# A graph-attention kernel: 18 targets instead of 20 summed early, and eight projection steps for each instead of seven

## The chip, the cores and the metric

The kernel runs on one core of a Trainium2 chip. The metric is the device time of one execution in microseconds (us); the time before is the median of six executions. The engines are TensorE (PE: matmuls, and PEld: its weight loads), VectorE (DVE), ScalarE (ACT), GpSimd (POOL) and SyncE (SP). Each engine works through its own queue of instructions in order, and waits for others by semaphores. Transfers (DMA) are issued from the queues of SP, ACT and POOL and share 16 DMA engines. The schedule in this kernel is written by hand: the order in which the Python code emits instructions is the order in each queue.

## What is computed

Two layers of graph attention over 3327 nodes with 1024 features, each followed by a residual and a normalisation. The adjacency matrix is sparse (about 16 neighbours for each node).

```python
def _L0_gnn_ref(x, adj, W, a_src, a_dst):          # 8 heads of 128
    h = (x @ W).reshape(C, H, D)
    e = alpha_src[:, :, None] + alpha_dst[:, None, :]
    e = where(e >= 0, e, 0.2 * e); e = where(adj[None] == 0, -inf, e)
    attn = softmax(e, axis=-1)
    return einsum('hij,hjd->hid', attn, h_heads)   # concatenated heads
def _L1_gnn_ref(input, adj, W, a1, a2):            # one head of 1024
    h = input @ W
    e = leaky_relu(h @ a1 + (h @ a2).T, 0.2); scores = where(adj > 0, e, neg)
    return relu(softmax(scores, axis=1) @ h)
x = _layernorm(x + _L0_gnn_ref(x, adj, ...))
x = _layernorm(x + _L1_gnn_ref(x, adj, ...))
```

## The kernel before

Nodes are cut into 26 tiles of 128 rows (`NT = 26`, `NTH = 13`). A tile of nodes that receives is called a target. The kernel makes, for each target, lists of its neighbours on DVE, and then gathers the neighbours' rows from a table in HBM with indirect transfers on POOL's queue. The neighbours of a target are put into blocks: blocks 0 and 1 hold neighbours out of tiles 0 to 12 (the near half), blocks 2 and 3 those out of tiles 13 to 25, and an end block holds what didn't fit. A block is four gathers of 128 rows, the end block one.

**Projection.** For every tile, PE makes h = x W in three pieces of columns, eight matmuls each (L578); ACT copies them out and SP stores the row of 1048 values (1024 features, a one for each head and two factors for each head) into the table `h0_d`. Tile t+1's third piece, with the scores, comes before its first two. Beside the matmuls run two generators, moved on by `pace()`, which is called after every second matmul of a piece, so 12 times for a tile: `listing()` makes the neighbour lists (seven steps a tile, paced by a line over the slots), and from tile 13 on `sums_so_far()`, one step at each pace.

**Early sums.** `sums_so_far()` computes the near half of layer 0's sums for the first `EARLY` = 20 targets, while the projection of tiles 13 to 25 goes on: the near half's rows are all in the table by then. There are 11 steps of preparation. Then, for each target and each of its two near blocks, three steps: `fetch(n + 2)` puts out the gathers of the block two ahead into one of three buffers (`near0`, `near1`, `far`; L696), `marks` (L704) and `weights` (L713, L714, L717) are DVE work, `sums` is PE work in two halves of 16 matmuls (L726; each appears as two instructions), and ACT scales the target's own row (L755), which an ACT-issued transfer brought. After the second block `settle` (L759) adds the three banks of sums to the own row on DVE, SP loads the lists of the target after the next, and a seventh step ends the target. SP stores the row into `half_d` in the next target. At target 12 `own_terms(NTH, EARLY)` makes the own factors of the rest. The loop also fetches the near blocks of target `EARLY` for the next stage. After the last tile, a loop runs out what is left of both generators.

**Rest of layer 0.** `sparse()` goes through all 26 targets. An early target needs its two far blocks and the end block (9 gathers) and loads its half sum from `half_d`; the 6 late targets need all five blocks (17 gathers) and load the own row from `h0_d`. The order is one late target, then five early ones, four times, then the last two late targets. Gathers (L1082) go out as the five block buffers come free. DVE makes weights (L1157 to L1160), PE sums (L1183, end block L1175, own rows L1172), then follow the division, the normalisation and the store of y.

**Layer 1** gathers rows of y the same way (17 gathers a target), sums on PE (L1283) and multiplies by the second weights (L1315).

`FIRST` names the targets whose lists hold a valid row in every place, as they fill buffers for the first time: 0, 1 and the first two late ones.

Of the kernel before, what the change touches and what calls it, by code (L numbers as in the profile page):

```python
# [26 lines left out]
def kernel(  # L27
# [35 lines left out]
    NTH = NT // 2  # L63
# [23 lines left out]
    HB = EB // 2  # L87
    HG2 = HB * P
    THR = NTH * P
    EARLY = NTH + 7  # L90
    FIRST = 0, 1, EARLY, EARLY + 1
    XN, XR, XL = 1, 2, 2 + H
    XB = XL + KMAX
# [41 lines left out]
    row_d = [scratch.tile([1, P], F32, name=f"row_d{t}") for t in range(NT)]  # L135
    half_d = [scratch.tile([P, DW], F32, name=f"half_d{t}") for t in range(EARLY)]
    io_t = const.tile([P, P], F32, name="io_t")
# [5 lines left out]

    own_e = const.tile([P, EARLY, H], F32, name="own_e")

# [396 lines left out]
    with ExitStack() as own, tc.manual_schedule():  # L542
# [140 lines left out]
        def sums_so_far():  # L683

            src = [near[0], near[1], far]
            k = EARLY * HB % 3
            src = src[-k:] + src[:-k] if k else src
            bound = nc.gpsimd.to_reg(THR - 1)

            def fetch(n):  # L690
                s, b = divmod(n, HB)
                if s > EARLY:
                    return
                for g in range(NG):
                    k = b * NG + g
                    nc.gpsimd.indirect_dma_start(  # L696
                        out=src[n % 3][:, g, :], out_offset=None, in_=h0_d[:THR, :],
                        in_offset=bass.IndirectOffsetOnAxis(ap=idx[:, s, k : k + 1], axis=0),
                        bounds_check=bound, oob_is_err=False,
                    )  # L700

            def marks(s):
                oh = part.sbuf("oh", [P, HB * NG, GT], 2)
                nc.vector.tensor_tensor(  # L704
                    oh, io_t[:, :GT].unsqueeze(1).to_broadcast([P, HB * NG, GT]),
                    tgt[:, s, : HB * NG].unsqueeze(2).to_broadcast([P, HB * NG, GT]), OP.is_equal,
                )
                return oh

            def weights(val, b, re, oh):  # L710
                blk = slice(b * NG, (b + 1) * NG)
                w = part.sbuf("w", [P, NG, H], 4)
                nc.vector.tensor_tensor(w, val[:, :, DW : DW + H], re[:, blk, :], OP.mult)  # L713
                nc.vector.tensor_tensor(w, w, val[:, :, DW + H :], OP.max)  # L714
                e = part.sbuf("e", [P, H * P], 2).rearrange("p (g h t) -> p g h t", g=NG, h=H)
                wide = [P, NG, H, GT]
                nc.vector.tensor_tensor(  # L717
                    e, oh[:, blk, :].unsqueeze(2).to_broadcast(wide), w.unsqueeze(3).to_broadcast(wide), OP.mult
                )
                return e  # L720

            def sums(acc, val, b, e, heads_):
                vals = val[:, :, :DW].rearrange("p g (h d) -> p g h d", h=H)
                for h in heads_:
                    for g in range(NG):
                        nc.tensor.matmul(  # L726
                            acc[h // 3][g * GT : (g + 1) * GT, h % 3, :], e[:, g, h, :], vals[:, g, h, :],
                            start=b == 0 and h in HEADS, stop=b == HB - 1 and h + 1 in HEADS,
                        )

            def listed(s):
                re = part.sbuf("re", [P, HB * NG, H], 3)
                nc.sync.dma_start(re, re_d[s][:, : HB * NG, :])
                return re

            def own_terms(lo, hi):

                mid = ph.sbuf("bits", [P, 8, KMAX], 1, dt=I32).rearrange("p a b -> p (a b)").bitcast(F32)
                m, e = (hi - lo) * H, own_e[:, lo:hi, :]
                mids = [mid[:, n * m : (n + 1) * m].rearrange("p (t h) -> p t h", h=H) for n in range(2)]  # L740
                for n, scale in enumerate((1.0, SLOPE)):
                    nc.scalar.activation(mids[n], sd0[:, lo:hi, 1, :], AF.Exp, scale=scale)
                nc.scalar.activation(e, sd0[:, lo:hi, 0, :], AF.Exp, scale=1 - SLOPE)
                nc.vector.tensor_tensor(e, e, mids[0], OP.mult)
                nc.vector.tensor_tensor(e, e, mids[1], OP.max)
                nc.vector.tensor_tensor(e, e, loop[:, lo:hi].unsqueeze(2).to_broadcast([P, hi - lo, H]), OP.mult)

            def own_row(s):
                if s < EARLY:
                    nc.scalar.dma_start(own_rows[s % 3], h0_d[s * P : (s + 1) * P, :DW])  # L750

            def scale(s, heads_):
                for h in heads_:
                    d = by_head(own_rows[s % 3])[:, h, :]
                    nc.scalar.activation(d, d, AF.Copy, scale=own_e[:, s, h : h + 1])  # L755

            def settle(s, acc, n):
                d = by_head(own_rows[s % 3])[:, HEADS[n] : HEADS[n + 1], :]
                nc.vector.tensor_tensor(d, acc[n], d, OP.add)  # L759

            def store(s):
                nc.sync.dma_start(half_d[s], own_rows[s % 3])
# [19 lines left out]
            for s in range(EARLY):  # L782
                acc = [part.bank("L", [P, HEADS[n + 1] - HEADS[n], DH1], "part") for n in range(3)]
                for b in range(HB):
                    n = s * HB + b
                    val, last = src[n % 3], b == HB - 1
                    if n:
                        fetch(n + 2)
                    yield
                    if last and s + 1 < EARLY:  # L790
                        oh = marks(s + 1)
                    yield
                    if s and b == 0:
                        store(s - 1)
                    sums(acc, val, b, e, range(H // 2))
                    scale(s, range(b * H // 2, b * H // 2 + 2))
                    yield
                    sums(acc, val, b, e, range(H // 2, H))
                    if last:
                        res.pop(0)  # L800
                    if n + 1 < EARLY * HB:
                        e = weights(src[(n + 1) % 3], (b + 1) % HB, res[0], oh)
                    scale(s, range(b * H // 2 + 2, (b + 1) * H // 2))
                    if last:
                        own_row(s + 2)
                if s == NTH - 1:
                    assert scored.issuperset(range(EARLY))
                    own_terms(NTH, EARLY)
                for n in range(3):
                    settle(s, acc, n)  # L810
                if s + 2 < EARLY:
                    res.append(listed(s + 2))
                yield
# [113 lines left out]
        for t in range(3, NT):  # L927
# [24 lines left out]
            if t == NTH:  # L952
                soon.append(sums_so_far())
# [641 lines left out]
```

## Time and profile before

| | |
|---|---|
| median of 6 executions | 1775.02 us (1770.69 to 1779.56) |
| profiled execution | 1768.09 us, span 1766.4 us, mean granted clock 0.945 |
| busy share of the span | PE 87%, PEld 49%, DVE 65%, POOL 59%, ACT 27% |
| transfers | 595.95 MB, mean 337 GB/s; 459.23 MB on POOL's queue |
| first early gather / first gather of the next stage | 233.1 us / 575.4 us |
| last matmul of the projection ends | 569.3 us |
| first gather of layer 1's rows | 1033.2 us |
| ends of the sums of the late targets | 621.6, 724.0, 829.5, 930.8, 1038.3, 1059.7 us |

The profile is one execution, and its times are counted from the start of the span. Busy shares are averages over stages that differ, so each stage has to be read by itself; a line such as L726 is a line of the kernel. A wait line reads "engine line <- who released it: us in total, times, longest". Idle time in front of an instruction is put down to the semaphore that came last.

### The profile page before, as it was taken

What the parts mean: (1) busy time and instruction counts of PE and PEld (TensorE: products, weight loads), DVE (VectorE), ACT (ScalarE), POOL (GpSimd) and SP (SyncE); (2) the same over time, 40 slices, a digit from 0 to 9 for tenths busy, and PEclk for the clock granted to TensorE, in tenths of its full rate; (3) what the DMA queues carried; (4) which work ended last, traced back from release to release, by engine and by line L of the source; (5) the groups of instructions that cost most, each with busy time, mean ns of one, the idle gap of its engine ahead of it and who ended that gap; (6) DMA issues with size and microseconds to landing.
All of it is one profiled execution on the core that took longest, in us unless ns stands there. A gap on an engine that the chain in (4) does not pass through costs nothing.

```text
span 1766.4 us, 33978 instructions
## 1 busy us (share of the span) xinstructions
PE 1543.8 (87%) x12635; PEld 859.8 (49%) x12635; DVE 1147.2 (65%) x3111; ACT 474.1 (27%) x1396; POOL 1045.1 (59%) x1311
## 2 busy tenths in 40 slices
PE   9799989999998478777767674999999999999998
PEld 5566656565565345454544441444444444444443
DVE  6699998898886778786877763343434444343443
ACT  5677753343333112222221221111101111110110
POOL 4433256676665666666666664666666666666650
PEclk9899999999899698898988997999999999999999
DMA  7699989999899999999999997999999999999980
GB/s 184 121 160 168 185 267 375 363 398 396 328 380 348 369 376 409 394 399 382 396 395 374 407 387 288 371 381 380 381 355 386 381 371 373 368 386 388 357 334 36
DMA packets 190320, 595.95 MB, mean 337 GB/s; under 512 B 37914, under 2 KB 47924, under 8 KB 190146
## 3 DMA queue, kind: packets, MB, share of 16 engines
q0 software_dynamic: 131056, 459.23, 73.2%
q1 hardware_dynamic: 56052, 123.63, 19.1%
q10 hardware_dynamic: 3038, 10.83, 1.6%
q8 instruction: 102, 1.67, 0.4%
q14 instruction: 72, 0.59, 0.1%
HBM read 593.53 MB, written 54.99 MB: 367 GB/s over the span
## 4 chain that ended last, share of the span: by engine, by line
PE 51%; DVE 11%; DMA 10%; issue 7%; ACT 1%; POOL 0%; DVEq 0%; SPq 0%; another core or an unknown queue 0%; POOLq 0%; ACTq 0%
PE mm L1315 21%; PE acc L1283 15%; PE acc L1183 7%; DMA src<-h_d,idx 3%; PE acc L1172 2%; PE acc L1175 2%; PE mm L578 1%; PE tr L206 1%; PE part L726 1%; DMA re_d<-re 1%; DMA near<-h_d,idx 1%; DMA own<-h_d 1%; DVE e L1160 1%; DVE top L322 1%; DVE pr L1048 1%
## 5 line engine op out<-in xcount | busy, mean ns | idle before, releaser
L578 PE MATMUL mm<-wt,xT 128*128 128x384 f32 (+1 forms) x1248 | 410.5, 473 | 0.6 <-issue 0.5
L1315 PE MATMUL mm<-wt,xT 128*128 128x512 f32 x832 | 388.8, 605 | 1.6 <-issue 1.4
L1082 POOL DMA_INDIRECT src<-y_d,idx x248 | 250.1, 1009 | 142.8 <-PE acc L1283 63.9
L578 PEld LDWEIGHTS mm<-wt,xT 128*128 128x128 f32 x1248 | 228.9, 193 | 125.8 <-issue 31.5
L1318 DVE SCALAR_TENSOR_TENSOR o<-mm,y 128x512 f32<-128x512 f32 x52 | 36.0, 692 | 336.3 <-PE acc L1283 131.4
L1315 PEld LDWEIGHTS mm<-wt,xT 128*128 128x128 f32 x832 | 149.4, 189 | 202.1 <-issue 197.2
L1082 POOL DMA_INDIRECT near<-y_d,idx x168 | 169.3, 1008 | 83.9 <-PE acc L1283 33.7
L1082 POOL DMA_INDIRECT src<-h_d,idx x152 | 159.5, 1049 | 89.2 <-PE acc L1183 42.6
L1183 PE MATMUL acc<-src,e 128*32 128x129 f32 x2432 | 135.2, 309 | 64.9 <-issue 43.8
L1283 PE MATMUL acc<-src,es 128*32 128x341 f32 x1488 | 138.2, 471 | 25.3 <-DVE es L1274 20.8
L696 POOL DMA_INDIRECT near<-h_d,idx x112 | 122.8, 1096 | 53.8 <-issue 24.0
L1082 POOL DMA_INDIRECT near<-h_d,idx x96 | 104.9, 1092 | 66.5 <-PE acc L1183 36.6
L1183 PEld LDWEIGHTS acc<-src,e 128*32 128x32 f32 x2432 | 87.4, 122 | 113.8 <-issue 84.3
L1183 PE MATMUL acc<-near,e 128*32 128x129 f32 x1664 | 86.4, 300 | 51.1 <-issue 31.7
L1160 DVE TENSOR_TENSOR e<-oh,way 128x1024 f32<-128x1024 f32 x90 | 109.9, 1221 | 26.6 <-PE acc L1183 14.7
L1297 ACT ACTIVATE z<-y,ri 128x342 f32<-128x342 f32 (+1 forms) x78 | 39.5, 570 | 318.0 <-issue 107.6
L209 ACT ACTIVATE xT<-tr 128x512 f32<-128x512 f32 x52 | 31.1, 597 | 268.6 <-PE tr L206 151.2
L1283 PEld LDWEIGHTS acc<-src,es 128*32 128x32 f32 x1488 | 51.0, 112 | 101.2 <-issue 61.5
L1183 PEld LDWEIGHTS acc<-near,e 128*32 128x32 f32 x1664 | 58.1, 119 | 81.6 <-issue 68.0
L1283 PE MATMUL acc<-near,es 128*32 128x342 f32 (+1 forms) x1008 | 88.7, 455 | 3.1 <-DVE es L1274 2.0
L696 POOL DMA_INDIRECT far<-h_d,idx x56 | 63.4, 1133 | 36.6 <-PE part L726 21.2
L415 ACT ACTIVATE junk<-ad 128x1664 uint8<-128x1664 uint8 x52 | 83.1, 1597 | 6.9 <-POOL ad L404 5.3
(236 smaller groups left out, 2336.3 us busy)
## 6 DMA issues: line engine op xcount, KB each, us to landing
y_d<-y SPq DMA_DIRECT2D x26, 514.0 KB
y<-y_d SPq DMA_DIRECT2D x26, 514.0 KB
xT<-in_x_t_dram SPq DMA_DIRECT2D x26, 512.0 KB
h_d<-ht SPq DMA_DIRECT2D x25, 524.0 KB
y<-in_x_dram SPq DMA_DIRECT2D x25, 512.0 KB
out_dram<-o SPq DMA_DIRECT2D x25, 512.0 KB
ad<-in_adj_dram POOLq DMA_DIRECT2D x25, 415.9 KB
own<-half_d SPq DMA_DIRECT2D x20, 516.0 KB
```

Source lines behind the costliest of these rows:

```text
L415: nc.scalar.activation(junk, ad[:, n * THR : (n + 1) * THR], AF.Copy, accum_out=self.d[:, n : n + 1])
L578: nc.tensor.matmul(accs[t, c], xT[t][:, k, :], wt[:, k, CUTS0[c] : CUTS0[c + 1]], start=k == 0, stop=k == KT - 1)
L696: nc.gpsimd.indirect_dma_start(out=src[n % 3][:, g, :], out_offset=None, in_=h0_d[:THR, :], in_offset=bass.IndirectOffsetOnAxis(ap=idx[:, ...
L1082: nc.gpsimd.indirect_dma_start(out=s[:, g, :w], out_offset=None, in_=table[:n, :], in_offset=bass.IndirectOffsetOnAxis(ap=idx[:, t, b * NG ...
L1160: nc.vector.tensor_tensor(e, oh.unsqueeze(2).to_broadcast([P, ng, H, wide]), wp.unsqueeze(3).to_broadcast([P, ng, H, wide]), OP.mult,)
L1172: nc.tensor.matmul(self.acc[n].rearrange("p h d -> p (h d)"), ident, part, start=False, stop=False)
L1175: nc.tensor.matmul(self.acc[h // 3][:, h % 3, :], e[:, 0, h, :], rowsof[:, 0, h, :], start=False, stop=h + 1 in HEADS,)
L1183: nc.tensor.matmul(self.acc[h // 3][g * GT : (g + 1) * GT, h % 3, :], e[:, g, h, :], rowsof[:, g, h, :], start=j == 0 and h in HEADS, stop ...
L1283: nc.tensor.matmul(self.acc[c][to, :m], es[:, g, :], s[:, g, CUTS[c] : CUTS[c + 1]], start=b == 0, stop=b == EB,)
L1297: nc.scalar.activation(z[:, cut], self.res[:, cut], AF.Copy, scale=ri[:, 1:2])
L1315: nc.tensor.matmul(acc, xT[:, k, :], wt1[:, k, half], start=k == 0, stop=k == KT - 1)
L1318: nc.vector.scalar_tensor_tensor(o[:, half], acc, 0.0, res[:, half], op0=OP.max, op1=OP.add)
```

## The change

The number of targets summed early goes from 20 to 18, and a further `yield` in `sums_so_far()` makes the adding up (`settle`) and the load of the next lists a step of their own, one pace after the second half of the second block's matmuls: eight steps for a target.

```diff
     THR = NTH * P
-    EARLY = NTH + 7
+    EARLY = NTH + 5
     FIRST = 0, 1, EARLY, EARLY + 1
...
                 if s == NTH - 1:
                     assert scored.issuperset(range(EARLY))
                     own_terms(NTH, EARLY)
+                yield
                 for n in range(3):
                     settle(s, acc, n)
                 if s + 2 < EARLY:
                     res.append(listed(s + 2))
                 yield
```

By `EARLY`, targets 18 and 19 become late ones. The rest of layer 0 then has eight late and 18 early targets, in the order of one late and three early ones, six times, then the last two late ones. The buffers of the early sums are rotated so that target 18's near blocks fall into `near0` and `near1` (the rotation is by 36 mod 3 = 0 in place of 40 mod 3 = 1).

## The prediction
> **What bounds the kernel now.** I read the stages first: busy time of each engine by stretch, with the stretches cut where the kernel changes its work. The span has four parts: projection alone (to about 246 us), projection with early sums beside it (to about 570), the rest of layer 0 (to about 1065), layer 1 (to the end). Columns: busy us of PE, weight load, DVE, ACT and POOL (each with its count), granted clock, DMA share, GB/s.
>
> ```profile
> core 0: us, PE busy (x) PEld busy (x) DVE busy (x) ACT busy (x) POOL busy (x), PEclk, DMA share, GB/s
> 170.00:246.00 76.00, 74.40 (x312) 48.62 (x312) 70.59 (x206) 57.32 (x157) 26.05 (x66) 1.00 1.00 189
> ...
> 276.50:415.25 138.75, 128.59 (x1486) 82.17 (x1490) 124.64 (x332) 52.37 (x218) 96.03 (x131) 0.99 1.01 385
> 415.25:551.80 136.55, 125.45 (x1406) 78.94 (x1402) 116.75 (x311) 48.35 (x195) 84.25 (x109) 0.96 0.96 365
> 276.50:551.80 275.30, 254.05 (x2884) 161.11 (x2888) 241.40 (x642) 100.72 (x411) 180.28 (x239) 0.98 0.98 375
> 551.80:575.00 23.20, 18.20 (x214) 11.13 (x214) 11.79 (x33) 8.78 (x40) 11.22 (x14) 0.94 0.91 326
> 575.00:1065.00 490.00, 350.89 (x4709) 236.32 (x4709) 369.99 (x920) 102.77 (x228) 313.45 (x296) 0.87 1.01 390
> ```
>
> With early sums PE is 92% busy, DVE 88% and DMA moves 375 GB/s: three resources are near full together. In the rest of layer 0 PE is 72% and DVE 76% busy while 390 GB/s flow. The DMA share of 1.00 says little: it is 1.00 at 189 GB/s too. GB/s decides.
>
> Next, who waits in the stage with early sums (us in total, times, longest).
>
> ```profile
> DVE w L713 <- DMA near<-h_d,idx: 5.9, 6, 3.0
> DVE kq L523 <- ACT xs L509: 3.7, 1, 3.7
> ...
> DVE w L713 <- DMA far<-h_d,idx: 2.4, 2, 1.3
> DVE ad L759 <- ACT ad L755: 1.8, 1, 1.8
> DVE ad L759 <- PE part L726: 1.7, 2, 1.5
> ```
>
> DVE waits for gathered rows in 8 of its about 34 blocks, 8.3 us out of 275. The chain of waits in this stretch runs mostly along DVE (listing steps and weights), in shorter pieces along PE, and three times over a transfer (7.6, 9.7 and 9.5 us). In the order of time, DVE instructions follow each other at 0.02 to 0.05 us; one tile of projection takes 27.5 us (ten copies of scores from 276.5 to 551.8), against 15.4 before the sums begin. So DVE and PE set this stage and transfers come close behind.
>
> For the rest of layer 0 I took one cycle of its order, one late target and five early ones, between two ends of an early run:
>
> ```profile
> 724.00:829.50 105.50, 78.81 (x1053) 52.15 (x1045) 79.48 (x202) 23.01 (x50) 67.56 (x62) 0.89 1.01 393
> 829.50:930.75 101.25, 73.86 (x1024) 51.27 (x1024) 79.74 (x203) 22.89 (x50) 65.56 (x61) 0.88 1.01 391
> ```
>
> No engine is over 80% and every cycle moves 391 to 395 GB/s. Bytes check it: an early target gathers 9 times, a late one 17; a gather of 128 rows of 4192 B is 0.537 MB, of which 0.95 move (the software queue's 459 MB less 11 MB of masks, over the 470 MB of 884 full gathers). With own rows, x, lists and the stored row (about 1.6 MB) that is 6.2 and 10.3 MB, for five and one 41.3 MB; 105.5 us at 393 GB/s are 41.5. So transfers bound this stage. Layer 1 is PE at 98% and the change doesn't touch it.
>
> **The change, part by part.** Two targets (18 and 19) leave the early sums and become late ones.
>
> *Removed from the projection.* The costs are in these groups (busy, mean ns | idle):
>
> ```profile
> L717 DVE TENSOR_TENSOR e<-oh,w 128x1024 f32<-128x1024 f32 x40 | 49.0, 1226 | 2.7
> L726 PE MATMUL part<-near,e 128*32 128x129 f32 x1664 | 61.6, 278 | 10.3 <-issue 4.9 <-DVE e L717 4.7 <-DVE ad L759 0.2
> L726 PE MATMUL part<-far,e 128*32 128x129 f32 x896 | 39.9, 288 | 8.5 <-issue 5.2 <-DVE e L717 3.0
> L759 DVE TENSOR_TENSOR ad<-part,ad 128x387 f32<-128x387 f32 (+1 forms) x42 | 19.4, 508 | 10.4 <-PE part L726 6.9 <-ACT ad L755 3.6
> L704 DVE TENSOR_TENSOR oh<-io_t,tgt 128x256 f32<-128x256 f32 x20 | 8.3, 416 | 0.0
> ```
>
> PE: (61.6+39.9)/20 = 5.1 us a target, 10.2 for two. DVE a target: marks 0.42, weights 2 x (1.23 + two small products of 0.19 and 0.20), adding up (19.4+8.2 for the group on the other buffer)/20 = 1.38; 5.0 us, 10.0 for two. Bytes a target: 8 gathers 4.10 MB, own row in and sum out 0.52 each, lists 0.03; 5.16, 10.3 for two. POOL loses 16 gathers of 1.3 us with their gaps, 21 us; it is 65% busy and sets nothing. The projection thus shortens by at least about 10 us (DVE or PE sets it throughout; less would need a new wait) and at most 10.3 MB at 375 GB/s = 27.5 (transfers set it throughout). The waits of DVE for rows stand nearer the first; I take 12: the 10 and a fifth of the transfer waits.
>
> *The added step.* It lies between the second half of the sums and the adding up, so the three adds of a target reach DVE one step (2.3 us) after PE got its last matmuls. They wait 6.9 us for PE and 3.6 for ACT over the whole stage; 5.2 of the first stand at the very last target, so at most some 6 us vanish. Nothing else waits longer: the list loads and the row store on SP come one step later with it, and the next own row on ACT's queue is issued before it. I take 3. What is late next is the weights of the following block, behind the listing steps.
>
> *The pacing.* Projection gives 152 paces (tiles 13 to 25, 12 each, 8 in the last). Before: 11 steps of preparation and 20 x 7 = 151. After: 11 + 18 x 8 = 155. Three steps no longer lie beside projection: 32 of target 17's matmul pairs (2.2 us of PE by the 1.09 us of a half), its adds (1.4) and its store. They drain behind the last listing step. The store is the catch: in the profile the first POOL instruction of the next stage waited 6.6 us for the last transfer out of the old stage's buffers, and a store of such size took 7.6 in the chain. The two gathers for the first late target go out three steps later as well. From 0 (all beside the about 10 us of change-over that exist) to 8 (a buffer of the next stage waits for the store); I take 2.5, the adds and part of the matmuls. No gain can come here, as only work is added.
>
> *Added to layer 0.* Two targets with five blocks for three: 16 more gathers, 8.2 MB, the own row read from another table with the same size. At 393 GB/s 20.9 us. If transfers were not the limit there, PE would set the price: (135.2+86.4 us of the two L1183 groups)/64 blocks = 3.46 us, times four blocks = 13.8. Less, or a gain, is excluded since both are real work in a stage with no idle transfer time. I take 20.9, since the cycles agree with the bytes within 1%. The new order, late and three early in place of late and five, moves no more bytes.
>
> The granted clock was 0.98 where the matmuls were and 0.87 where they go; a block took 2.54 us there and takes 3.46 here. The Trainium skill (TensorE: Matmul & The Clock Gate, Part 1: The HAM clock gate) says an idling array is throttled and activity releases it, which speaks against the move; as transfers cover PE there, this row does not enter the sum. On transfers, the rows show 390 to 395 GB/s; the skill (DMA: Bandwidth & Descriptors, Specifications) gives about 358 as a core's HBM share and 435 as the fabric's ceiling. An estimate by that page would be 22.9 or 18.9 us for the 8.2 MB; the trace already exceeds the first.
>
> **Sum:** -12 - 3 + 2.5 + 20.9 = +8.4 us. The profiled execution took 1768.1 us (span 1766.4), which is 6.9 below the median 1775.0 and below the lowest run; I put the difference on the median: 1783.4.
>
> **Rivals.**
> 1. *Transfers set the projection (the other side).* Place: gathers of near rows at L696. For it: 385 to 405 GB/s over most of 276 to 450, the three transfers on the chain, and gathers that POOL could issue only when PE released a buffer. Against it: DVE's short waits for rows. Then 27.5 go, with the 3 of the adds: -27.5 - 3 + 2.5 + 20.9 = -7.1, 1768. It decides from a projection shorter by over 27 us.
> 2. *The change-over pays in full.* The store and late gathers hold the next stage, and the projection only loses its 10 us: -10 + 8 + 20.9 = +18.9, 1794. For it: the 6.6 us wait. Against it: the profile doesn't show which buffers of the next stage lie where the row buffers were, and PE and DVE drain together in some 4 us.
> 3. *Layer 0 absorbs part.* Cycles with three early targets leave DVE and PE more even, and the two targets cost 13.8: -15 + 2.5 + 13.8 = +1.3, 1776. Against it: the even 391 to 395 GB/s.
>
> **How the numbers follow.** A measurement of this kernel tells about 0.2%, 3.5 us, from no change. Forecast (about +4 to +14) 0.43, rival 2 0.17, rival 3 and other near-balances 0.17, rival 1 0.23. So slower 0.60, same 0.17, faster 0.23. The range goes from rival 1 to rival 2, 1768 to 1794, and leaves out about 0.08 on each side.
>
> **What would show it.** In the changed profile the tile period with early sums should fall from 27.5 to about 26.3 us, DVE still over 85% busy, and GB/s there fall to about 350; if GB/s stays at 375 and the period goes below 25.2, rival 1 holds. Layer 0 should last 490 + 21 us at 390 GB/s; at 504 or less rival 3 holds. Between the last projection matmul and the first gather of the next stage (now 6 us) over 5 us more means rival 2. I am wrong if DVE's waits for rows vanish and PE then runs without a gap, since the projection could give nearly the whole 21 us back.

## The result, and the profile after

The changed kernel took 1782.45 us (median of 20 runs) against 1773.34 for the kernel before (46 runs): a ratio of 1.0056, 95% interval 1.0046 to 1.0065, about 9 to 10 us more. The forecast was +8.4 us, and the time lies 1 us from the forecast one. The terms of that sum were off by 2 to 4 us each, not all in one direction, so the stages have to be compared one by one.

First the busy times by stretch of the changed kernel, cut at the same events as in the prediction, with its columns: from the tenth copy of scores before the last to the last, on to just ahead of the next stage's first gather, and from there to 5 us behind the last sum of layer 0.

```profile
278.60:533.64 255.04, 239.60 (x2593) 152.75 (x2592) 226.96 (x615) 95.32 (x393) 152.43 (x220) 0.99 0.96 354
533.64:565.00 31.36, 20.67 (x246) 12.70 (x244) 13.94 (x45) 10.27 (x45) 14.81 (x18) 0.92 0.82 300
565.00:1078.00 513.00, 376.48 (x4965) 251.90 (x4965) 375.55 (x930) 107.14 (x243) 326.07 (x312) 0.86 1.01 391
```

Ten tiles of projection with early sums take 255.0 us in place of 275.3, and transfers fall from 375 to 354 GB/s there, while PE rises from 92 to 94% busy and DVE from 88 to 89%. The rest of layer 0 takes 513 us in place of 490 at the same rate (391 and 390 GB/s), and the stretch between the two is 8 us longer. Next, what DVE waited for in the ten tiles.

```profile
DVE kq L523 <- ACT xo L512: 11.0, 7, 3.7
DVE w L713 <- DMA far<-h_d,idx: 3.0, 1, 3.0
DVE w L713 <- issue: 1.1, 1, 1.1
DVE w L713 <- DMA near<-h_d,idx: 0.4, 1, 0.4
```

The waits for gathered rows shrink from 8.3 to 3.4 us, and those of the adds (L759) for PE and ACT are gone, as the added step meant. The waits for ACT's copies of the lists (L523) grow, from 5.1 to 11.0 us. Last the change-over, DVE's and POOL's instructions of the changed kernel in order of time (lines after 808 are one higher than before).

```profile
556.02 1.35 DVE L759 TENSOR_TENSOR own<-part,own 128x387 f32<-128x387 f32 x3
563.01 0.12 DVE L1036 MEMSET y<- 128x4 f32 x3 [5.64 <-DMA half_d<-own]
```

```profile
553.90 1.00 POOL L696 DMA_INDIRECT near<-h_d,idx  x1 [0.30 <-issue]
563.41 1.96 POOL L1028 MEMSET end<- 128x1048 f32 x2 [8.51 <-DVE y L1037]
565.52 1.00 POOL L1083 DMA_INDIRECT src<-h_d,idx  x1 [0.15 <-issue]
```

The adds of target 17 run behind the projection, then DVE waits 5.6 us for the store of that row before it may write the first buffer of the next stage, and POOL waits for DVE. From the last projection matmul (ends 551.4) to the next stage's first gather are 14.1 us. In the kernel before it was 6.1, with POOL waiting for a store of lists:

```profile
573.32 1.91 POOL L1027 MEMSET end<- 128x1048 f32 x2 [6.60 <-DMA re_d<-re]
575.39 1.01 POOL L1082 DMA_INDIRECT src<-h_d,idx  x1 [0.15 <-issue]
```

Eight us more is rival 2's mark.

By stages, in us: from the scores of tile 13 to the end of the projection, on to DVE's first division for the first late target (L1195, within 3 us of the end of its sums), on to the first matmul with layer 1's weights. The last column is an average tile with early sums (from the scores of tile 15 to those of tile 25; tiles without sums at the end of some kernels are in it).

| kernel (one execution each) | projection | change-over | rest of layer 0 | tile |
|---|---|---|---|---|
| before / after | 336.9 / 318.2 | 52.2 / 59.1 | 488.1 / 511.0 | 27.5 / 25.5 |
| n19_seven | 328.4 | 50.5 | 502.1 | 27.2 |
| n21_seven | 359.5 | 59.9 | 479.1 | 27.9 |
| half_rows | 351.2 | 53.0 | 493.0 | 28.6 |
| no_adds | 340.1 | 52.4 | 487.8 | 27.7 |
| base / changed (other chip) | 336.4 / 309.7 | 49.6 / 56.7 | 483.2 / 501.8 | 27.6 / 25.0 |
| seven_k | 336.0 | 51.0 | 480.0 | 27.5 |
| late_half | 308.6 | 56.1 | 476.4 | 24.9 |
| n18_seven | 319.7 | 49.2 | 499.6 | 26.5 |
| n18_eight_early | 319.5 | 49.0 | 502.6 | 25.8 |
| n18_mixed | 310.2 | 54.7 | 481.6 | 25.1 |
| n20_eight | 311.1 | 78.6 | 481.7 | 25.1 |

The experiments ran in three sets, each on one chip: one where the kernel before takes 1775.0 us, close to the result's 1773.3 (n19_seven, n21_seven, half_rows, no_adds), and two where it takes 1729.2 (the n18 kernels and n20_eight) and 1728.7 (base, changed, seven_k, late_half). Ratios are to the kernel before on the same chip. n18_eight_early, n18_mixed and late_half start from the changed kernel, the others from the kernel before. One execution scatters: half_rows and no_adds have the rest of layer 0 of the kernel before, and differ by 5 us in it. In the first row the stages add up to +11.1, and the two executions differ by 14.9 us where the medians differ by 9.1; base and changed add up to -1.0 where the times say +3.4. So the stages are good to some 5 us.

### The profile page after: what moved, and what is told of

Read it like the earlier page. It is cut to its first block, busy times and chain, and to the rows that moved or that the text cites. A ratio compares the mean times of both kernels' runs of the same rounds, so it can differ in the third digit from the quotient of the medians.

```text
span 1781.3 us, 33967 instructions
## 1 busy us (share of the span) xinstructions
PE 1560.2 (88%) x12635; PEld 870.5 (49%) x12635; DVE 1142.9 (64%) x3109; ACT 473.3 (27%) x1396; POOL 1033.1 (58%) x1311
## 4 chain that ended last, share of the span: by engine, by line
PE 52%; issue 8%; DMA 4%; DVE 3%; POOL 0%; ACT 0%; SPq 0%; DVEq 0%; another core or an unknown queue 0%; POOLq 0%; ACTq 0%
PE mm L1316 21%; PE acc L1284 14%; PE acc L1184 9%; PE acc L1176 3%; PE acc L1173 3%; DMA own<-h_d 2%; PE tr L206 1%; DMA near<-h_d,idx 1%; DMA src<-h_d,idx 1%; DVE e L1161 1%; DMA end<-y_d,idx 0%; DVE pr L1208 0%; DMA src<-y_d,idx 0%; DVE pr L1049 0%; DVE y L1201 0%
## 5 line engine op out<-in xcount | busy, mean ns | idle before, releaser
L1083 POOL DMA_INDIRECT src<-y_d,idx x256 | 257.5, 1006 | 149.0 <-PE acc L1284 69.0
L1083 POOL DMA_INDIRECT src<-h_d,idx x160 | 168.8, 1055 | 95.3 <-PE acc L1184 48.2
L1083 POOL DMA_INDIRECT near<-y_d,idx x160 | 162.6, 1016 | 82.6 <-PE acc L1284 35.7
L1184 PE MATMUL acc<-src,e 128*32 128x129 f32 x2560 | 142.2, 297 | 65.8 <-issue 56.9
L1284 PE MATMUL acc<-src,es 128*32 128x342 f32 (+1 forms) x1536 | 140.3, 471 | 25.5 <-DVE es L1275 22.3
L1083 POOL DMA_INDIRECT near<-h_d,idx x104 | 108.4, 1043 | 67.8 <-PE acc L1184 35.2
L696 POOL DMA_INDIRECT near<-h_d,idx x104 | 110.7, 1064 | 61.3 <-PE part L726 34.0
L1161 DVE TENSOR_TENSOR e<-oh,way 128x1024 f32<-128x1024 f32 x94 | 114.8, 1221 | 38.0 <-PE acc L1176 22.3
L1184 PE MATMUL acc<-near,e 128*32 128x129 f32 x1792 | 92.5, 293 | 49.8 <-issue 38.9
L1173 PE MATMUL acc<-own,ident 128*128 128x387 f32 (+1 forms) x156 | 73.0, 576 | 7.7 <-ACT own L1143 4.9
```

Of the source, the lines that this page charges most:

```text
L696: nc.gpsimd.indirect_dma_start(out=src[n % 3][:, g, :], out_offset=None, in_=h0_d[:THR, :], in_offset=bass.IndirectOffsetOnAxis(ap=idx[:, ...
L1083: nc.gpsimd.indirect_dma_start(out=s[:, g, :w], out_offset=None, in_=table[:n, :], in_offset=bass.IndirectOffsetOnAxis(ap=idx[:, t, b * NG ...
L1161: nc.vector.tensor_tensor(e, oh.unsqueeze(2).to_broadcast([P, ng, H, wide]), wp.unsqueeze(3).to_broadcast([P, ng, H, wide]), OP.mult,)
L1173: nc.tensor.matmul(self.acc[n].rearrange("p h d -> p (h d)"), ident, part, start=False, stop=False)
L1184: nc.tensor.matmul(self.acc[h // 3][g * GT : (g + 1) * GT, h % 3, :], e[:, g, h, :], rowsof[:, g, h, :], start=j == 0 and h in HEADS, stop ...
L1284: nc.tensor.matmul(self.acc[c][to, :m], es[:, g, :], s[:, g, CUTS[c] : CUTS[c + 1]], start=b == 0, stop=b == EB,)
```

## The experiments

**n18_seven: the number of targets alone.**

```diff
-    EARLY = NTH + 7
+    EARLY = NTH + 5
```


> 18 targets, without the added step: 11 + 126 = 137 steps, all beside projection. My theory (the work taken out of the projection gives about 16 us, the rest of layer 0 costs 21 to 22, and the changed kernel's further 8 us are the last store draining behind the projection): change-over back to about 6 us, +3 to +7 us against the kernel before. Rival (the number of targets alone makes the whole loss, the step and its tail are harmless): as the changed kernel, +9 to +10.


Ratio 1.0024 (1.0012 to 1.0037), +4.2 us, within my range. The change-over is 49.2 us: without left-over steps it doesn't grow. But on a chip of the same time the changed kernel takes +3.4 us (below), not the +9 to +10 that I had set against it. So the rival fits as well: the number of targets makes the whole loss here, and the added step with its tail costs or gains nothing that could be told from noise. The 8 us that I gave to the draining store don't show as a loss.

**n18_eight_early: the added step, and all of it inside the projection.**

```diff
             res = [listed(0), listed(1)]
-            for _ in range(3):
-                yield
             own_terms(0, NTH)
```


> The changed kernel with the three empty steps of preparation taken out, so that 8 + 144 = 152 steps fit the 152 paces. My theory: the change-over falls from 14 to 6 or 7 us, so about 7 us less than the changed kernel, +1 to +4 against the kernel before. Rival (the change-over is long for another reason than the store): +8 to +10, as the changed kernel.


Ratio 1.0043 (1.0027 to 1.0060), +7.4 us: a miss, just under the rival's range and 4 us over the changed kernel on a chip of the same time. The change-over did fall, from the 56.7 of changed to 49.0, but the projection took 319.5 in place of 309.7. Of these 9.8 us, 2.2 are at the start (the scores of tile 13 to those of tile 15: 46.0 us, in the other kernels on its chip 43.7 to 43.9), and for the rest the work of three steps is now inside. So the left-over steps cost about what they cost beside the projection; a longer change-over is no loss by itself, as rival 2 had booked it.

**n18_mixed: the two sides of the balance apart.**

```diff
+    PART = EARLY + 2
...
-                    nc.sync.dma_start(self.h[:, :DW], half_d[self.t])
+                    half = half_d[self.t] if self.t < EARLY else h0_d[self.t * P : (self.t + 1) * P, :DW]
+                    nc.sync.dma_start(self.h[:, :DW], half)
```
`PART` stands for `EARLY` in `FIRST`, in `sparse()` and in the list that the last fetches of the early sums use.


> Leaves out the near sums of targets 18 and 19: projection as in the changed kernel (18 targets, eight steps), rest of layer 0 as in the kernel before (20 early targets, own rows of 18 and 19 read from the first table). It parts the two sides of the balance. My theory: projection and change-over give -8 to -11 us against the kernel before, and the two targets cost 20 to 22 us in layer 0, by transfers. Rival (layer 0 is set by PE, 14 us for two targets, and the projection gives only 5): -3 to -5 us.


Ratio 0.9890 (0.9871 to 0.9909), -18.5 us: a miss. Projection and change-over give more than I had expected. Against changed (+3.4 on a chip of the same time) the two late targets cost 21.9 us in the rest of layer 0, as worked out from the bytes (20.9), not 13.8.

**n20_eight: the added step alone.**

```diff
                 if s == NTH - 1:
                     assert scored.issuperset(range(EARLY))
                     own_terms(NTH, EARLY)
+                yield
```


> The added step alone, with 20 targets: 171 steps, of which 19 do not fit and run after the projection. My theory: the projection is shorter by about as much as in the changed kernel (18 to 21 us), but 2.4 targets then run alone at 10 to 13 us each and the change-over waits for the last store: +12 to +20 us. Rival (the added step itself frees DVE, and what overflows hides in the change-over): within 5 us of the kernel before.


Ratio 1.0038 (1.0026 to 1.0050), +5.9 us: a miss on the good side, close to the rival. The added step alone is no gain. The projection is 25.3 us shorter than base's and the change-over 29.0 longer. Nineteen steps outside the projection cost little more than inside.

**n19_seven and n21_seven: one target less, one more.**

```diff
-    EARLY = NTH + 7
+    EARLY = NTH + 6        # n19_seven
+    EARLY = NTH + 8        # n21_seven, with 5 steps of preparation in place of 11
```


> 19 targets, no added step: 11 + 133 = 144 steps, all beside projection. My theory (each target taken out gives 8 to 9 us in the projection and costs 10.5 to 11 in the rest of layer 0): +1 to +4 us against the kernel before. Rival (transfers set the projection, 13.7 us a target): -3 us.


Ratio 1.0019 (1.0000 to 1.0038), +3.4 us, as expected: the projection gives 8.5, the rest of layer 0 takes 14.0 more in this execution.


> 21 targets, with the preparation cut from 11 to 5 steps so that 5 + 147 = 152 fit. My theory: one target more costs 8 to 9 us in the projection and saves 10.5 to 11 in layer 0: -1 to -4 us. Rival (transfers set the projection): +3 us. A further case: if the last store then ends just behind the last pace, some of the 8 us of the change-over appear and eat the gain.


Ratio 1.0090 (1.0071 to 1.0108), +16.5 us: a miss. The rest of layer 0 falls by 9.0, as it should. The projection grows by 22.6, of which 15.5 between the scores of tiles 13 and 15 (59.6 us in place of 44.1). The longest waits of PE and DVE there:

```profile
PE part L726 <- DVE e L717: 9.3, 1, 9.3
DVE wd L420 <- POOL ad L404: 5.1, 1, 5.1
```

PE waits for the first weights, and DVE, which makes them after its list steps, waits for a list step of POOL (L404) that stands behind eight gathers issued without a pause. The empty steps of preparation are the cover of the first gathers and lists, and I had taken them for spare. The change-over is 7.7 us longer, which my further case had named. So this kernel doesn't tell what a 21st target costs by itself.

**half_rows: the bytes of the projection.**

```diff
+                m = HG if s == EARLY else HG // 2
...
-                        out=src[n % 3][:, g, :], out_offset=None, in_=h0_d[:THR, :],
+                        out=src[n % 3][:, g, :m], out_offset=None, in_=h0_d[:THR, :],
```
(and the three buffers are filled with ones at tile 12.)


> The kernel before, with the early near gathers bringing the first 524 of 1048 columns only (the other columns hold ones; 2.05 MB a target left out): 41 MB less in the projection, engines' work unchanged. My theory (DVE and PE set the projection): -5 to -15 us, only the waits for rows go. Rival (transfers set it): -25 us or more, down to where PE is full. The rest of layer 0 unchanged in both.


Ratio 1.0100 (1.0081 to 1.0119), +17.5 us: outside both ranges. The same stretch of both kernels, before first:

```profile
290.00:540.00 250.00, 232.56 (x2613) 147.47 (x2605) 218.53 (x582) 93.34 (x380) 162.75 (x223) 0.97 0.98 374
```

```profile
290.00:540.00 250.00, 229.42 (x2511) 143.09 (x2510) 207.01 (x554) 89.67 (x366) 157.28 (x215) 0.97 0.71 226
```

Transfers drop from 374 to 226 GB/s and the tiles get no shorter. DVE's waits for rows (7.3 us there in the kernel before) are gone, and a wait that was 1.4 us takes their place:

```profile
DVE kq L523 <- ACT xo L512: 16.2, 7, 4.3
```

Seven us are lost before tile 13, where the filling was put; why the tiles are 1.1 us longer I can't say. But rival 1, transfers that set the projection, is gone.

**no_adds: DVE's work in the projection.**

```diff
-                for n in range(3):
-                    settle(s, acc, n)
```


> The kernel before without the adding up of the early sums to the own rows (L759 left out, 27.6 us of DVE work over the projection). My theory (DVE sets much of the projection): -12 to -25 us. Rival (transfers set it): 0 to -5 us. If PE alone sets it: 0 to -5 us too, then half_rows tells which.


Ratio 0.9999 (0.9984 to 1.0015): nothing.

```profile
290.00:540.00 250.00, 234.23 (x2628) 149.15 (x2627) 197.03 (x531) 92.66 (x380) 162.38 (x220) 0.96 0.98 368
```

DVE falls from 87 to 79% busy, and its waits take the time instead (15.5 us for near rows and 15.9 for ACT's copies of the lists, before 4.9 and 1.4). DVE by itself doesn't set this stage: my theory up to here fell, and PE was next.

**base, changed and seven_k: PE's work, and the stages on one chip.** base and changed are the kernels before and after as they stand; the edit is seven_k's.

```diff
-                        accs[t, c], xT[t][:, k, :], ..., start=k == 0, stop=k == KT - 1
+                    top = KT - (t > NTH)
+                    if k == top:
+                        continue
...
+                        accs[t, c], xT[t][:, k, :], ..., start=k == 0, stop=k == top - 1
```


> The kernel before, unchanged, for a profile from the same chip as the changed kernel's: 0 us within the scatter of single runs.

> The changed kernel on the same chip: +8 to +11 us. By stages against base, if the reading so far holds: start of tile 13 to the end of the projection -16 to -20 us, from there to the end of the first late target's sums +3 to +7 (the drained tail), from there to the start of layer 1's matmuls +18 to +23 (transfers at 393 GB/s). If the change-over is small here, the changed kernel's long change-over was an accident of one execution.

> The kernel before, leaving out the eighth part (k = 7) of the projection's matmuls of tiles 14 to 25, with the same paces: 12 tiles x 3 x 2 instructions of 0.28 to 0.35 us, 23 us of PE. half_rows and no_adds were not faster than the kernel before, so my reading that DVE sets the projection fell; what is left is PE. If PE sets it: -17 to -25 us. Rival (no engine sets it by itself, each waits in turn for steps of another in the order of the queues): 0 to -8 us.


base, one execution, took 1733.4, 4.7 over the median of its set. changed: ratio 1.0018 (1.0001 to 1.0034), +3.4 us: a miss. The loss is smaller here, as the projection gives 26.7 us (the table) where I had 16 to 20; the other two stages are within or at my ranges, and the long change-over is there again. seven_k: ratio 1.0002 (0.9985 to 1.0018), nothing, as the rival had it. base first, then seven_k:

```profile
280.00:540.00 260.00, 238.15 (x2787) 154.39 (x2789) 228.72 (x610) 99.28 (x405) 173.08 (x231) 0.97 0.99 376
```

```profile
280.00:540.00 260.00, 224.61 (x2691) 144.10 (x2691) 227.59 (x611) 97.42 (x400) 167.81 (x231) 0.95 0.99 376
```

PE has 13.5 us less to do in 260 and idles them: a tile takes 27.5 us as before. PE by itself isn't the limit either.

**late_half: the bytes of the rest of layer 0.**

```diff
+            if table is h0_d and b < HB:
+                w = w // 2
```


> The changed kernel, with the near blocks of the late targets gathered at half width in the rest of layer 0 (the other columns stay from earlier gathers): 56 gathers at 0.25 MB less each, 14.3 MB; the engines' work is unchanged. If transfers set layer 0 at 394 GB/s: 36 us less than the changed kernel, -26 us against the kernel before. Rival (the engines' order sets it): as the changed kernel, +5 to +10.


Ratio 0.9850 (0.9816 to 0.9884), 28.1 us less than changed, of the 36 expected; the rest of layer 0 is 25.4 shorter. changed first, then late_half:

```profile
640.00:1000.00 360.00, 230.43 (x3637) 178.28 (x3632) 271.34 (x685) 80.19 (x180) 233.71 (x219) 0.82 1.01 395
```

```profile
640.00:1000.00 360.00, 238.44 (x3931) 185.15 (x3927) 285.80 (x725) 85.97 (x195) 249.66 (x232) 0.84 1.00 384
```

Fewer bytes, more instructions in the same time: transfers set this stage. Three quarters of the 36 us appear; the rate falls to 384 GB/s, so by then something else is late part of the time.

## Why the prediction was right, point by point

- *The rest of layer 0, +20.9.* Right in mechanism and size: 22.9 and 18.6 us in the two pairs of traces, 21.9 by times (n18_mixed against changed), the rate 391 to 396 GB/s between 600 and 1060 us in the kernels with 18, 19 and 20 early targets, and late_half shows the cause. (One reading under it was too even: the fourth cycle of the kernel before, 930.75 to 1038.3 us, moved 385 GB/s, not 391 to 395.)
- *Removed from the projection, -12.* The sign was right, the size too small: n18_seven, which has this term alone, is 17.1 us shorter than base in projection and change-over. The step that failed is the reasoning under it, "DVE or PE sets it throughout". Part of PE's matmuls, DVE's adds or the bytes, each taken away by itself, gave nothing (seven_k, no_adds, half_rows), so the price of a target can't be read off one engine's row. Removing a target takes work from every queue at once, and that paid: 8.4 us a target in the projection of n18_seven (16.7 for two) and 8.5 in n19_seven, where PE's and DVE's rows had 5.
- *The added step, -3, and the pacing, +2.5 (0 to 8).* The waits of the adds went, and a tile fell to 25.5 and 25.0 us where I wrote 26.3. The change-over grew by 6.9 and 7.1, near the upper bound, by the very wait for the store that was named. But n18_eight_early shows that it isn't a loss of its own: the projection is shorter by the steps that it no longer carries. Both terms together were -0.5. From n18_seven to changed they are -2.5 in the stages and -0.8 by times, which is not clear of noise, and n20_eight, the step alone, took 5.9 us more than the kernel before. So a gain of 3 us from the step is not shown.
- *The projection's side as a whole.* -15 + 2.5 = -12.5 predicted, -11.8 in the first pair, -19.6 in the second, and -18.5 by the times of n18_mixed.
- *The rivals.* Rival 1 named the wrong cause (half_rows), though a projection shorter by almost its 27 us did occur in the second pair. Its sign came half: the tile fell under 25.2 us there, but the rate fell to 360 GB/s too, where it had to stay at 375. Rival 2's sign appeared without its price. Rival 3 fell by the 21.9 us and by late_half.
- *The sum.* +8.4 was met by +9 to 10 on the first chip; on the second chip +3.4. Part of this was luck. On the first chip the gain was larger than I said, and the tail and layer 0 took it back. On the second the projection nearly gave back what layer 0 cost, which the prediction had named as its way of being wrong; by the time of that chip the forecast would be 5 us off.

What stays open is what sets a tile with seven steps a target at 27.5 us. It stood at 27.5 to 28.6 with 40% of the transfer rate, a tenth of DVE's or a seventeenth of PE's work taken away, one at a time. Either PE and DVE are near enough to full that removing from one leaves the other, or the waits of ordered queues for each other (ACT for PE's list matmuls, DVE for ACT, PE for ACT and DVE) set it; a kernel with less of both at once would tell, and wasn't tried. None of the runs was faster than the kernel before with the whole work done, and 18, 19 and 20 targets lie within 10 us.

## What to carry to other kernels

When work is moved between two stages, price it in the receiving stage by what bounds that stage (here bytes over a steady rate, right within 2.3 us), and in the giving stage not by one engine's rows when several engines are about 90% busy: take one whole unit of work away and measure. What drains behind a stage is no extra cost if the stage got shorter by it; book both ends in one term. Steps that look empty at the start of a pipeline may be the time that its first transfers need.

## What the runs showed of the hardware

The kernel before took 1729 us in two sets of runs and 1773 to 1775 in the others. The traces show a difference: in the longer ones PE pauses for 0.3 to 1.1 us inside its blocks of small matmuls, often after three to five of them, for nothing that the profile shows; in the shorter ones it doesn't. From the rest of layer 0 (655 to 1000 us), PE's largest wait in after and in n18_seven, both with 18 targets:

```profile
PE acc L1184 <- issue: 70.3, 158, 1.1
```

```profile
PE acc L1183 <- DVE e L1160: 106.2, 30, 5.4
```

PE was busy 260 of 345 us with the pauses and 220 without, and 394 GB/s flowed in both. So this stage didn't get much shorter (488.1 us in before, 483.2 in base). Layer 1, where PE is 99% busy, did: from its first matmul with the second weights to the end of the span 657 us in before, 630 in base. There the pauses hardly show as waits (3.1 us from 1130 to 1700 us in before), but the same small matmuls of gathered rows (L1283, from 1115 to 1730 us) are busy 203.8 us in before and 185.5 in base. The cause was not looked for. Nor does the DMA share follow the rate: it fell to 0.71 at 226 GB/s in half_rows, and was 1.00 at 189 GB/s in the projection alone.
